# Attention and mixture of experts: the stretch between the last router step and the first expert slot, reordered

## The chip, the cores and the metric

The kernel runs on one core of a Trainium2 chip. A core has a matrix engine (TensorE, PE in the profile, with its weight loads shown as PEld), a vector engine (VectorE, DVE), a scalar engine with function tables (ScalarE, ACT), a general engine (GpSimd, POOL) and an engine that mainly starts transfers (SyncE, SP). Each engine works through its own instructions in order and waits on semaphores for the others. Data lies in on-chip memory of 128 partitions (SBUF); matmuls write into PSUM.

The metric is the time of one execution on the device in microseconds. The profile is of a single execution; the timed runs are others.

## The reference

Everything is float32. There are 32 sequences of 100 tokens with 256 features, and for each sequence 361 context rows with 192 features.

```python
x = x + cross_attention(layernorm(x), ctx)       # softmax over 361 context rows
z = layernorm(x)
shared = gelu(z @ ws1 + bs1) @ ws2 + bs2         # one shared block, all tokens
aff = softmax(z @ Wr + br)                       # 31 experts
vals, idx = top_k(aff, 3)
routed = sum over the 3 chosen experts e of
         aff[e] * (gelu(z @ We1[e] + Be1[e]) @ We2[e] + Be2[e])
x = x + (shared + routed + z)
```

## The kernel before

**Tiles and blocks.** The 3200 tokens are 25 tiles of 128 (`NT`); four tiles make a block, so there are seven blocks, the last with one tile (`BLOCKS`, `TPB = 4`). Inside the part in question the order on the engines is written out by hand (`tc.manual_schedule`, L78): what a line issues stands in its engine's queue where the program puts it.

**Attention and router steps (L796 to L879).** A loop of 37 steps pipelines the sequences: at step i it loads, normalises and transposes one context, forms scores of the one before, weights the one before that. A token tile t is projected out of attention at step `at(t)`, normalised one step later, gets its router logits two steps later (`route_turn`, `route_logits`, `route_choice`) and its slots three steps later (`route_gates`, `route_count`, `route_slots`, `route_scatter`). The last steps, 33 to 36, have no attention left to speak of: step 34 has the logits of tile 23 and the slots of tile 22, step 35 the logits of tile 24 and the slots of tile 23, step 36 the slots of tile 24. `route_count` (L665) counts by matmuls how many earlier tokens chose each expert; for tile 24 it also gives the totals from which `cnt` (31 counts) comes (L685). `route_scatter` writes rows to DRAM by indirect transfers on GpSimd.

**The shared block.** `shared_half(k, f, psum)` (L716) forms one half of the hidden layer of block k: four matmul records with 512 columns into a PSUM tile. `shared_gelu(k)` (L725) applies the gelu to both halves. `shared_mm(t)` (L740) takes tile t through the second matrix, with the experts' second biases by gates as a third matmul (six records of 256 columns), into `pys`; `shared_add(t)` (L750) adds that to the tile. PSUM tiles come from one pool with two tags of four buffers each: `ps_t` ("tp") and `ps_m` ("mm").

**From counts to slots (L887 to L981).** From the 31 counts each expert's number of slots (128 rows each) is formed, `nt_i`, and its running sum, `ends`: a cast into a padded buffer (L898) and five shifted adds between two buffers `runs` (L900 to L904), whose 16 leading zeros were written at the start (L411). From `ends` each of up to 105 slots finds its expert `ei`, the number of slots before that expert `st0`, and its first row (L909 to L925). Two transposes (`p_ec`, L930) turn the expert number and first row of each slot from a column into a row. VectorE makes integers of it (`eT`, read by SyncE's registers, which start the loads of weights and rows) and packs four expert numbers into one word (`epT`, read by TensorE's registers). Then `shared_mm(0)` and `shared_mm(1)` stand on TensorE (L944, L945), while VectorE forms two diagonal matrices; their product with ones (`p_bc`, L954) brings per-slot numbers to all partitions. A one-hot matrix is transposed (`p_oh`), the hidden biases of each slot are picked (`p_b1`), and between these stand the other `shared_mm` and the `shared_add` of block 0.

**Slots.** `fetch` starts the transfers for four slots at a time: weights and scattered rows. After the register loads (`registers`, L1106), `shared_second(1)` does the second matrix of block 1 (L1117); then `run(0, NU)` takes 92 slots: two transposes, eight matmul records, gelu, four more, and an indirect store of the rows. At the end the stored rows are collected and summed, beside the shared blocks 2 to 6.

Of the kernel before, what the change touches and what calls it, by code (L numbers as in the profile page):

```python
# [8 lines left out]
F32 = mybir.dt.float32  # L9
# [4 lines left out]
ALU = mybir.AluOpType  # L14
# [21 lines left out]
def xattn_ffn(  # L36
# [5 lines left out]
    nc = tc.nc  # L42
    P = 128
    EPS = 1e-5
    B, L1, D1 = x.shape
    L2, D2 = ctx_in.shape[1], ctx_in.shape[2]
    E = Wq.shape[1]
    NE, _, INTER = We1.shape
    NG = NE + 1
# [20 lines left out]
    const = ctx.enter_context(tc.tile_pool(name="const", bufs=1))  # L70
# [15 lines left out]
    def ps_t(name):  # L86
        return ps.tile([P, 512], F32, tag="tp", name=name)
# [46 lines left out]
    def load_ctx(b):  # L134
        z = zring[b % ZB]
        full = sum(1 for _, n in CH if n == P)
        nc.sync.dma_start(
            z[:, :full, :D2], ctx_in[b, : full * P, :].rearrange("(c p) d -> p c d", p=P)
        )
        for c in range(full, NCH):  # L140
            s, n = CH[c]
            nc.sync.dma_start(z[:n, c, :D2], ctx_in[b, s : s + n, :])
        ztile[b] = z
# [5 lines left out]
    def load_x(t, n):  # L149
        k, j = divmod(t, TPB)  # L150
        nc.sync.dma_start(
            xb[k][:, j : j + n, :], xf[t * P : (t + n) * P, :].rearrange("(t p) d -> p t d", p=P)
        )
# [18 lines left out]
    b2z = const.tile([P, TPB, D1], F32, tag="b2z", name="b2z")  # L172
# [72 lines left out]
    def ctx_rough(g):  # L245
        n = len(CG[g]) * NCH
        yc[g] = rough(vc[g], n, f"c{n}", f"c{g}")
# [20 lines left out]
    def token_rough(g):  # L268
        n, ts = len(XG[g]), slice(XG[g][0], XG[g][-1] + 1)
        v = small_t(n, f"xv{n}", f"x{g}", 1)  # L270
        pool.tensor_scalar(v, mv1[:, ts, 1], 4.0 * (1.0 + EPS), 4.0 * EPS * EPS, ALU.mult, ALU.add)
        yx[g] = v, rough(v, n, f"x{n}", f"x{g}")
# [94 lines left out]
    def iota_t(shape, name, pattern, base=0, mult=0, pool=const):  # L367
        t_ = pool.tile(shape, F32, tag=name, name=name)
        nc.gpsimd.iota(
            t_, pattern=pattern, base=base, channel_multiplier=mult, allow_small_or_imprecise_dtypes=True  # L370
        )
        return t_
# [4 lines left out]
    iota_p = iota_t([P, 1], "iota_p", [[0, 1]], mult=1)  # L377
# [7 lines left out]
    pool.memset(ones, 1.0)  # L385

    GM = 4
    PAD = 16
    iota0 = iota_t([P, NE], "iota0", [[1, NE]])
    dump = iota_t([P, P], "dump", [[P, P]], base=KTOP * T, mult=1)  # L390
    transposed(wq_sb, KD1, wqT, "q")
# [3 lines left out]
    for t in XG[0]:  # L395
# [5 lines left out]
    token_rstd(0)  # L401

    kk = iota_t([P, GM, KTOP], "kk", [[0, GM], [1, KTOP]])
    one, oh, onesf, *runs = (
        const.tile([P, n], F32, tag=name, name=name)
        for name, n in (("one", NE), ("oh", NG), ("onesf", P), ("run0", PAD + NE), ("run1", PAD + NE))
    )
    for t_ in (one, onesf):
        pool.memset(t_, 1.0)
    for t_ in (oh, b2z, *runs):  # L410
        pool.memset(t_, 0.0)  # L411

    mv2 = const.tile([P, NT, 2], F32, tag="mv2", name="mv2")
# [152 lines left out]
    def clear(k):  # L566
        first_, last_ = k * NE // CLEAR, (k + 1) * NE // CLEAR
        nc.sync.dma_start(
            xse[:, first_:last_, :], none[:, None, :].to_broadcast([P, last_ - first_, XW])
        )  # L570
        if k == 0:
            nc.sync.dma_start(xs_d[NE * T :, :], none)
# [33 lines left out]
    def route_rough(ts):  # L606
        v2[ts[0]] = v2[ts[0]], rough(v2[ts[0]], len(ts), f"m{len(ts)}", f"m{ts[0]}")
# [108 lines left out]
    def shared_half(k, f, psum):  # L716

        n = len(BLOCKS[k]) * P
        ph = phs[k, f] = psum(f"phs_{k}_{f}")
        for c in range(2):  # L720
            nc.tensor.matmul(  # L721
                ph[:, :n], ws1_sb[:, c, f::2], xT[k][:, c, :], start=(c == 0), stop=(c == 1)
            )

    def shared_gelu(k):  # L725
        n = len(BLOCKS[k]) * P
        h = hs[k] = shp.tile([P, 2, 512], F32, tag="hs", name=f"hs_{k}")
        for f in range(2):
            nc.scalar.activation(
                h[:, f, :n], phs.pop((k, f))[:, :n], AF.Gelu, bias=b1c[:, f, NE : NE + 1]  # L730
            )

    def shared_first(k):
        for f in range(2):
            shared_half(k, f, ps_m)
        shared_gelu(k)
# [3 lines left out]
    def shared_mm(t):  # L740
        k, j = divmod(t, TPB)
        h, py = hs[k], ps_t(f"pys_{t}")
        for f in range(2):
            nc.tensor.matmul(  # L744
                py[:, :D1], h[:, f, j * P : (j + 1) * P], ws2_sb[:, f, :], start=(f == 0), stop=False
            )
        nc.tensor.matmul(py[:, :D1], gT[k], b2z[:, j, :], start=False, stop=True)  # L747
        pys[t] = py
# [14 lines left out]
    def at(t):  # L763
        return 1 - (-(t + 1) * P // L1)
# [31 lines left out]
    for i in range(B + 5):  # L796
        now, norm, logits, slots = ([t for t in range(NT) if at(t) == i - d] for d in range(4))
        scattered = [t for t in range(EARLY * TPB) if at(t) == i - 4]
        for b in range(AHEAD - 2, AHEAD + 1) if i == 0 else [i + AHEAD]:
            if b < B:  # L800
                load_ctx(b)
        if i in loads:
            loads[i]()
        if i in xloads:
            load_x(*xloads[i])
        if 1 <= i <= CLEAR:
            clear(i - 1)
        for e in range((i - W2) * NE // (B - W2), min((i + 1 - W2) * NE // (B - W2), NE)) if i >= W2 else ():
            nc.sync.dma_start(w2r[:, e, :], w2v[:, e, :])

        if i + 1 in trstd:
            token_rough(trstd[i + 1])
        if i in trstd:
            token_rstd(trstd[i])
        if norm:
            route_rough(norm)
        if i in crough:
            ctx_rough(crough[i])
        if 2 <= i < B + 2:
            exp_transpose(i - 2)  # L820
        for t in slots:
            route_gates(t)
        if 1 <= i < B + 1:
            scores(i - 1)
        for t in logits:
            route_turn(t)
        for t in slots:
            route_count(t)
            route_slots(t)
            route_scatter(t)  # L830
            if i <= B:
                route_transpose(t)
        if i < B:
            ctx_transpose(i)
        if i in crstd:
            ctx_rstd(crstd[i])
        if i + 1 < B:
            ctx_normalise(i + 1)
        for b in cstats.get(i, ()):
            ctx_stats(b)  # L840
        if i == 0:
            ctx_rough(CGOF[2][0])
        for t in tstats.get(i, ()):
            token_stats(t)
        if norm:
            route_rstd(norm)
        for t in norm:
            route_norm(t)
        if 2 <= i < B + 2:
            weighted(i - 2)  # L850
        for t in projected(i + 2):
            token_norm(t)
        for t in logits:
            route_logits(t)
        for t in projected(i):
            token_project(t)
        for t in projected(i + 1):
            token_transpose(t)
        for t in logits:
            route_choice(t)  # L860
        for t in scattered:
            early_residual(t)
        for t in now:
            project_out(t)
        if now:
            route_var(now)
        if i == 0:
            transposed(wv_sb, KD2, wvT, "v")
        if i == 1:
            bias_cols(wv_sb, KD2, B2, BV, lambda ec: wvT[:, ec, D2:DA], "bvc")  # L870
        if i == 2:
            fold_values()
        if i == 5:
            shared_biases()

        if i == B + 1:
            shared_half(0, 0, ps_t)
        if i == B + 3:
            shared_half(0, 1, ps_t)  # L879
    residual_factors(slice(EARLY * TPB, NT))  # L880
    shared_gelu(0)
    shared_first(1)

    att_ctx.close()

# [3 lines left out]
    def sel_t(shape, name, dt=F32):  # L889
        return sel.tile(shape, dt, tag=name, name=name)  # L890
# [3 lines left out]
    nt_i = sel_t([P, NE], "nt_i", I32)  # L894
    nc.vector.tensor_scalar(nt_i, cnt_i, 7, None, ALU.logical_shift_right)
    ntf = sel_t([P, NE], "ntf")
    nc.vector.tensor_copy(ntf, nt_i)
    nc.vector.tensor_copy(runs[0][:, PAD:], nt_i)  # L898
    cur, step = 0, 1
    while step < NE:  # L900
        nc.vector.tensor_tensor(
            runs[1 - cur][:, PAD:], runs[cur][:, PAD:], runs[cur][:, PAD - step : PAD - step + NE], ALU.add
        )
        cur, step = 1 - cur, 2 * step  # L904
    ends = runs[cur][:, PAD:]
    ind = sel_t([P, NE], "ind")
    ei = sel_t([P, 1], "ei")
    st0 = sel_t([P, 1], "st0")
# [3 lines left out]
    nc.vector.scalar_tensor_tensor(ind, iota0, ei, cnt, ALU.is_equal, ALU.mult, accum_out=nn)  # L912

    j128 = sel_t([P, 1], "j128")
    nc.vector.tensor_tensor(j128, iota_p, st0, ALU.subtract)
    nc.vector.tensor_scalar(j128, j128, float(P), None, ALU.mult)
    start = sel_t([P, 1], "start")
    nc.vector.scalar_tensor_tensor(start, nn, float(-P), j128, ALU.add, ALU.min)
    nc.vector.tensor_scalar(start, start, 0.0, None, ALU.max)
# [20 lines left out]
        nc.vector.scalar_tensor_tensor(ep, e4[:, :, k], float(1 << (BITS * k)), ep, ALU.mult, ALU.add)  # L940
    epT = sel_t([1, P // PACK], "epT", I32)
    nc.vector.tensor_copy(epT, ep)

    shared_mm(0)  # L944
    shared_mm(1)  # L945


    diag = sel_t([P, 2 * P], "diag")
# [249 lines left out]
```

## Time and profile before

| what | us |
|---|---|
| runs, median of 3 (lowest to highest) | 505.77 (505.1 to 506.42) |
| the profiled execution: its time | 503.07 |
| the profiled execution: its span, first to last instruction | 501.2 |
| router steps 34 to 36 and the counts, until `p_ec` starts | up to 245.62 |
| `p_ec` to `p_bc` | 245.62 to 248.43 |
| `p_bc` to the first slot's transposes | 248.43 to 259.15 |

The span is what the trace covers; the time has some 1.9 us more around it. The mean granted TensorE clock over the span is 0.978 of full speed. The first part of the page gives each engine's busy time:

```profile
PE 455.3 (91%) x2952; PEld 397.2 (79%) x2952; DVE 312.4 (62%) x1281; ACT 249.2 (50%) x814; POOL 271.7 (54%) x544
```

A busy TensorE includes matmuls that run at a lower clock. The lines of a timeline below give the start in us from the span's start, the duration in us, the engine and source line, the operation with output and inputs, and in brackets the idle time of that engine just before, with what ended it.

### The profile page before, as it was taken

The numbers are of one execution on the slowest core, as the hardware profiler recorded it, in microseconds if no ns is written. First come the engines' busy times: TensorE is split into PE (matmuls) and PEld (weight loads), VectorE is DVE, ScalarE is ACT, GpSimd is POOL, SyncE is SP. The second block draws the span as 40 slices with busy tenths as digits, with TensorE's granted clock in tenths as the row PEclk, the third lists the DMA queues.
The fourth block names the chain that finished last, engine by engine and source line by source line (L and its number), as shares of the span: only waits on it lengthen the run. The fifth ranks groups of instructions, "written<-read, shape, count | busy, mean of one in ns | idle before, by whom it ended". The sixth has DMA issues, their size and how long they took to land. (4 is left out here: it accounts for less than half of the span.)

```text
span 501.2 us, 10979 instructions
## 1 busy us (share of the span) xinstructions
PE 455.3 (91%) x2952; PEld 397.2 (79%) x2952; DVE 312.4 (62%) x1281; ACT 249.2 (50%) x814; POOL 271.7 (54%) x544
## 2 busy tenths in 40 slices
PE   0989997998998999996999999999999999989964
PEld 0878785977887888885579999999999999966653
DVE  0489998798998887757644444444444434312995
ACT  0357686687877786853414444444444444432100
POOL 3334286877676666667604555555555555553750
PEclk9999999799999999999999999999999999999977
DMA  7864954353645741111387888898888888426982
GB/s 214 237 170 136 281 189 140 113 154 104 190 136 164 234 161 42 66 66 55 123 265 223 270 254 263 267 266 249 269 253 265 257 269 260 152 78 243 406 305 94
DMA packets 67784, 98.79 MB, mean 197 GB/s; under 512 B 8290, under 2 KB 43177, under 8 KB 67721
## 3 DMA queue, kind: packets, MB, share of 16 engines
q1 hardware_dynamic: 56348, 72.60, 50.0%
q0 software_dynamic: 8048, 22.17, 11.6%
q10 hardware_dynamic: 3324, 3.28, 1.9%
q8 instruction: 28, 0.46, 0.4%
q14 instruction: 36, 0.29, 0.2%
HBM read 68.27 MB, written 29.74 MB: 196 GB/s over the span
## 5 line engine op out<-in xcount | busy, mean ns | idle before, releaser
L551 POOL DMA_INDIRECT y_d<-ys,yrow x92 | 88.6, 964 | 100.0 <-ACT ys L1074 43.3
L1058 ACT ACTIVATE hT<-ph,b1t 128x128 f32<-128x128 f32 x184 | 57.7, 364 | 103.6 <-PE ph L1053 95.3
L1053 PE MATMUL ph<-xgT,w 128*128 128x128 f32 x736 | 101.8, 281 | 0.1
L1053 PEld LDWEIGHTS ph<-xgT,w 128*128 128x128 f32 x736 | 94.8, 197 | 0.4 <-DVE xgT L1045 0.3
L1068 PE MATMUL py<-w2r,hT 128*128 x368 | 94.3, 380 | 0.0
L551 POOL DMA_INDIRECT xs_d<-xl,su x75 | 75.1, 1001 | 27.4 <-issue 8.9
L1068 PEld LDWEIGHTS py<-w2r,hT 128*128 128x128 f32 x368 | 62.9, 190 | 4.8
L1076 DVE TENSOR_SCALAR ys<-py,gate 128x256 f32<-128x256 f32 x46 | 22.3, 484 | 65.2 <-PE py L1068 65.2
L1045 DVE COPY xgT<-pg 128x256 f32<-128x256 f32 x92 | 38.6, 421 | 33.5 <-PE pg L1043 33.4
L484 PE MATMUL pss<-z2T,qk 65*100 65x361 f32 (+1 forms) x128 | 44.9, 472 | 1.9 <-ACT qk L448 1.7
L513 PE MATMUL pcx<-exT,z 128*65 128x100 f32 (+3 forms) x384 | 44.3, 266 | 0.1
L513 PEld LDWEIGHTS pcx<-exT,z 128*65 128x65 f32 (+3 forms) x384 | 40.8, 168 | 0.7 <-ACT exT L500 0.6
L1043 PEld LDWEIGHTS pg<-ident,xg 128*128 128x128 f32 x184 | 35.6, 196 | 4.0
L1043 PE MATMUL pg<-ident,xg 128*128 128x128 f32 x184 | 35.5, 277 | 0.0
L744 PE MATMUL pys<-ws_sb,hs 128*128 128x256 f32 x100 | 27.7, 402 | 5.8 <-DVE x L752 4.8
L1139 POOL TENSOR_TENSOR y<-y 128x256 f32<-128x256 f32 x25 | 20.1, 804 | 17.8 <-DMA y<-y_d 12.6
L529 PE MATMUL po<-wvo,cT 128*128 128x257 f32 (+1 forms) x100 | 26.9, 391 | 3.1 <-ACT cT L520 2.8
L444 PE MATMUL pq<-zT,m_sb 128*128 128x128 f32 (+1 forms) x200 | 29.6, 294 | 0.0
L491 ACT ACTIVATE ex<-pss,nm 100x361 f32<-100x361 f32 x32 | 18.0, 563 | 22.0 <-DVE nm L489 18.9
L484 PEld LDWEIGHTS pss<-z2T,qk 65*100 65x100 f32 (+1 forms) x128 | 18.8, 167 | 12.1 <-ACT qk L448 3.3
L744 PEld LDWEIGHTS pys<-ws_sb,hs 128*128 128x128 f32 x100 | 19.7, 201 | 10.7 <-issue 8.0
L237 DVE BATCH_NORM_STATS2 stc<-z 128x6 f32<-128x192 f32 (+1 forms) x96 | 27.8, 345 | 0.0
(229 smaller groups left out, 865.8 us busy)
## 6 DMA issues: line engine op xcount, KB each, us to landing
w<-in_L_ffn_We_dram SPq DMA_DIRECT2D x92, 256.0 KB
xg<-xs_d SPq DMA_DIRECT2D x92, 131.5 KB
y<-y_d SPq DMA_DIRECT2D x25, 384.0 KB
w2r<-in_L_ffn_We_dram SPq DMA_DIRECT2D x31, 256.0 KB
z<-in_ctx_dram SPq DMA_DIRECT2D x32, 192.0 KB
xs_d<-none SPq DMA_DIRECT2D x3, 1052.0 KB
out_dram<-x ACTq DMA_DIRECT2D x6, 512.0 KB
x<-in_x_dram SPq DMA_DIRECT2D x5, 512.0 KB
```

Source lines behind the costliest of these rows:

```text
L237: nc.vector.bn_stats(st[:n, c, :], ztile[b][:n, c, :D2])
L444: nc.tensor.matmul(pq[:m, c * P : (c + 1) * P], m_sb[:, d, s : s + m], z[:, d, :], start=(d == 0), stop=(d == 1))
L484: nc.tensor.matmul(pss[:L1, :L2], qk[:m, a, b * L1 : (b + 1) * L1], z2T[:m, a, :], start=(a == 0), stop=(a == 1),)
L513: nc.tensor.matmul(pw[:m, :L1], z[:n, c, s : s + m], exT[:n, c, :], start=(c == 0), stop=(c == NCH - 1))
L529: nc.tensor.matmul(po[:, : D1 + 1], cT[:m, a, t * P % RING : t * P % RING + P], wvo[:m, a, :], start=(a == 0), stop=(a == 1))
L551: ins = nc.gpsimd.indirect_dma_start(out=dst, out_offset=bass.IndirectOffsetOnAxis(ap=index, axis=0), in_=src, in_offset=None).ins
L744: nc.tensor.matmul(py[:, :D1], h[:, f, j * P : (j + 1) * P], ws2_sb[:, f, :], start=(f == 0), stop=False)
L1043: nc.tensor.transpose(pt[:, c * P : (c + 1) * P], g[:, c::2], ident)
L1045: nc.vector.tensor_copy(xgT[i].rearrange("p c s -> p (c s)"), pt[:, : 2 * P])
L1053: nc.tensor.matmul(ph[:, f * P : (f + 1) * P], w1s[:, c, f::2], z[:, c, :], start=(c == 0), stop=(c == 1))
L1058: nc.scalar.activation(hT[i][:, f, :], ph[:, f * P : (f + 1) * P], AF.Gelu, bias=b1t[:, f, i : i + 1])
L1068: nc.tensor.matmul(py[:, :D1], h[:, f, :], w2f[:, bass.ds(e * (2 * D1) + f * D1, D1)], start=(f == 0), stop=(f == 1),)
```

## The change

Three things are changed.

- **The places of the shared halves.** Half (0, 1) goes from step 35 to step 34, half (1, 0) comes to step 35, and half (1, 1) stays behind the loop, after the gelu of block 0. The second-matrix matmuls of tiles 0 and 1 go from behind `epT` to a place ahead of the gelu of block 1, that is ahead of the counts' instructions and of `p_ec`.
- **The running sum.** The cast and the five shifted adds become one `tensor_tensor_scan` on VectorE over the 31 numbers (state times one, plus the next number). The two padded buffers and their zeroing on GpSimd go.
- **`j128`.** A subtraction and a multiplication become one instruction with two operations.

```diff
-    one, oh, onesf, *runs = (
-        const.tile([P, n], F32, tag=name, name=name)
-        for name, n in (("one", NE), ("oh", NG), ("onesf", P), ("run0", PAD + NE), ("run1", PAD + NE))
+    one, oh, onesf = (
+        const.tile([P, n], F32, tag=name, name=name) for name, n in (("one", NE), ("oh", NG), ("onesf", P))
     )
...
-    for t_ in (oh, b2z, *runs):
+    for t_ in (oh, b2z):
         pool.memset(t_, 0.0)
...
         if i == B + 1:
             shared_half(0, 0, ps_t)
+        if i == B + 2:
+            shared_half(0, 1, ps_t)
         if i == B + 3:
-            shared_half(0, 1, ps_t)
+            shared_half(1, 0, ps_m)
     residual_factors(slice(EARLY * TPB, NT))
     shared_gelu(0)
-    shared_first(1)
+    shared_half(1, 1, ps_m)
+    for t in range(2):
+        shared_mm(t)
+    shared_gelu(1)
...
-    nc.vector.tensor_copy(runs[0][:, PAD:], nt_i)
-    cur, step = 0, 1
-    while step < NE:
-        nc.vector.tensor_tensor(
-            runs[1 - cur][:, PAD:], runs[cur][:, PAD:], runs[cur][:, PAD - step : PAD - step + NE], ALU.add
-        )
-        cur, step = 1 - cur, 2 * step
-    ends = runs[cur][:, PAD:]
+    ends = sel_t([P, NE], "ends")
+    nc.vector.tensor_tensor_scan(ends, one, ntf, 0.0, ALU.mult, ALU.add)
...
-    nc.vector.tensor_tensor(j128, iota_p, st0, ALU.subtract)
-    nc.vector.tensor_scalar(j128, j128, float(P), None, ALU.mult)
+    nc.vector.tensor_scalar(j128, iota_p, st0, float(P), ALU.subtract, ALU.mult)
...
-    shared_mm(0)
-    shared_mm(1)
```

`B` is 32, so `B + 1` to `B + 3` are steps 33 to 35.

More of the change, by code (lines that the diff above doesn't have):

```diff
@@ L387, in xattn_ffn @@
     GM = 4
-    PAD = 16
     iota0 = iota_t([P, NE], "iota0", [[1, NE]])
```

## The prediction

> **What bounds the kernel now.** I first read the windows view over the stages, to see which engine fills each:
>
> ```profile
> 237.30:240.60 3.30, 3.30 (x5) 1.50 (x6) 1.50 (x8) 2.47 (x7) 2.81 (x6) 0.54 0.31 108
> 240.60:245.60 5.00, 4.11 (x15) 1.88 (x13) 3.84 (x25) 2.65 (x5) 4.15 (x9) 1.00 0.26 92
> 259.15:445.90 186.75, 186.61 (x1286) 177.58 (x1285) 83.17 (x316) 79.02 (x229) 95.85 (x178) 1.00 0.82 245
> ```
>
> Columns: the stretch in us, its length, busy us of PE, PEld, DVE, ACT and POOL, then the granted TensorE clock, the DMA share and GB/s. From 259.15 to 445.90 TensorE is busy 186.61 of 186.75 us, so the slot loop ends as much earlier as its first matmul starts. What follows (the last shared blocks, the sums) shifts with it. The question is therefore when TensorE reaches 259.15, and the first row shows something odd on that way: 3.3 us at a clock of 0.54. Next the timeline of PE from the last router step on (start, duration, engine, line, what; idle time before it and its releaser):
>
> ```profile
> 236.65 0.85 PE L630 MATMUL pr<-wr,qk 128*128 128x31 f32 x4 [0.54 <-ACT qk L624]
> 237.31 3.45 PE L721 MATMUL phs<-qk,ws_sb 128*128 128x512 f32 x4
> 240.60 0.30 PE L669 MATMUL pp<-sums,onesf 128*128 128x31 f32 x2
> ...
> 241.02 3.68 PE L721 MATMUL phs<-qk,ws_sb 128*128 128x512 f32 x8
> 245.62 0.38 PE L930 MATMUL p_ec<-ident,both 128*1 128x128 f32 x2 [0.91 <-DVE both L923]
> 245.83 1.03 PE L744 MATMUL pys<-ws_sb,hs 128*128 128x256 f32 x4
> ...
> 248.43 0.68 PE L954 MATMUL p_bc<-diag,onesf 128*128 128x256 f32 x2
> ```
>
> Up to p_ec the order is: half (0,1) of the shared block takes 3.29 us (237.31 to 240.60) where eight such matmuls take 3.5 us a little later, that is 1.75 us a half; the count matmuls of tile 24 wait behind it; DVE then runs the counts; p_ec waits 0.91 us for DVE. From p_ec on, pys 0 and 1 fill PE until p_bc at 248.43 (two times 1.30 us), just when DVE has its `diag` ready. From there to 259.15 PE has one gap, 1.05 us for its register loads. The DVE side of the same stretch:
>
> ```profile
> 241.21 0.25 DVE L681 TENSOR_TENSOR eq<-eq,pp 128x93 f32<-128x93 f32 x1 [2.01 <-PE pp L673]
> ...
> 242.39 0.18 DVE L897 CAST ntf<-nt_i 128x31 f32<-128x31 int32 x1
> 242.48 0.17 DVE L898 CAST run<-nt_i 128x31 f32<-128x31 int32 x1
> 242.69 1.09 DVE L901 TENSOR_TENSOR run<-run 128x31 f32<-128x31 f32 x5
> 243.81 0.25 DVE L909 SCALAR_TENSOR_TENSOR ind<-run,iota_p,one 128x31 f32<-128x31 f32 x1
> ...
> 246.03 0.41 DVE L932 CAST eT<-p_ec 1x256 int32<-1x256 f32 x1 [0.41 <-PE p_ec L930]
> ```
>
> Last, windows of 3.41 us, the length of the shortest spell of half clock here. Its boundaries (86.73, 236.92, 240.33, 482.68) all lie on one grid of 3.413 us:
>
> ```profile
> 83.32:86.73 3.41, 1.90 (x11) 1.09 (x9) 3.04 (x14) 1.74 (x8) 0.22 (x2) 1.00 0.46 122
> 151.58:154.99 3.41, 1.79 (x18) 1.82 (x19) 3.20 (x16) 1.76 (x6) 1.64 (x6) 1.00 0.13 47
> 233.51:236.92 3.41, 1.09 (x8) 0.83 (x8) 2.67 (x13) 1.45 (x7) 2.77 (x7) 1.00 0.21 67
> 236.92:240.33 3.41, 3.41 (x8) 1.86 (x8) 1.50 (x8) 2.20 (x7) 2.90 (x6) 0.50 0.28 99
> ```
>
> The first and third are windows after which the clock fell; the second is one after which it did not. So a window with PE about half busy is the border.
>
> **The change, step by step.**
>
> *Half (0,1) a step earlier.* At step 34 it comes behind the logits of tile 23, at about 233.0, and takes 1.75 us at the full clock which this place has. PE sat idle 1.51 us before the transposes of tile 24 (234.71); these slip to 234.95. That is hidden: ScalarE copies them only at 236.25, behind its gate scaling (L663, 236.04). If this cover were gone it would cost 0.25 us.
>
> *Half (1,0) at step 35* takes the old place of (0,1). With the filler before it, the clock should be full here: logits 0.2 us shorter, the half 1.75 instead of 3.29, together about 1.75 us. Count matmuls, L681 and all behind them come 1.75 us earlier: L681 at 239.45.
>
> *Running sums.* The cast (L898) and five adds (L901) go, a scan comes. From L897's start to L909's start is 1.42 us now. After: 0.22 us to the scan's start (the step between dependent ops in the rows above) and the scan. No scan is in the trace. Nearest row: L901, 191 ns each. [...] Ends: 0.19 by the row, 1.1 if it were as slow as the five adds. I take 0.22; with the step to L909 this saves about 0.9. The j128 merge saves one dependent op, 0.19. Together 1.1: `both` is ready at 245.56 - 1.75 - 1.1 = 242.7.
>
> *pys 0 and 1 ahead of p_ec.* They need the gelu of block 0. ScalarE starts its table load at 239.33, after L663, and that moves by 0.2 only; the two gelus end at about 241.1 and 241.7. PE meanwhile runs half (1,1) from 239.25 to 241.0. So pys 0 and 1 run from 241.1 (with about 0.2 us of wait for the second gelu) to 243.9, and p_ec, ready at 242.7, waits for them until 243.9: 1.7 us earlier than now. The DVE saving of 1.1 us is swallowed whole; it pays nothing unless the pys pair moves away. (This also covers a slow scan up to 1.2 us.)
>
> *Behind p_ec.* eT to the second `diag` stays 2.3 us on DVE, p_ec to p_bc 2.8 us as now. But now PE has nothing in between: after p_ec it idles some 2.55 us, to p_bc at 246.7 (-1.7).
>
> *PSUM turn.* If the four "tp" buffers go round in order of allocation, p_oh takes the buffer of pys 0 and pys 3 that of pys 1, each free only after its shared_add. L964 and three adds run at 249.61 to 250.86: the second add ends 2.08 us after p_bc, where pys 3 started 1.92 after it. Cost 0 to 0.4, I take 0.2, on the path.
>
> *DMA and POOL.* The scatters of tile 24 are bound by POOL and don't move (last issue 245.22, landing 2.4 to 2.8 us after: 248.0). SP starts the weights 1.7 us earlier and would reach the row loads at about 248.6, so that wait stays hidden. Two memsets of 0.14 us go from POOL at 19.1, ahead of 5.4 us of idle: nothing. The const tiles that go are 376 bytes per partition: no cost seen.
>
> Sum without the clock: -1.7 + 0.2 = **-1.5 us**.
>
> **The clock.** [...] The row 83.32 says otherwise: in that window the longest gap at the end was under 1.5 us, PE was busy 1.90 of 3.41, and the clock fell, with 1.79 busy it once did not. Taking "idle over 1.9 us in one window" from my count of the streaming time (0.43 of that window, 0.45 in the one that kept its clock), a gap of 2.55 us makes a window fall for (3.41 + 2.55 - 3.8)/3.41 = 0.63 of the positions of the grid. [...] The price: the next 3.41 us run at half, with PE dense from p_bc on: 2.7 to 3.4 us, half of it lost, 1.35 to 1.7, and the 0.2 of pys 3 disappears in it. I take the row, since it is measured here: -1.7 + 1.6 = **-0.1 us**.
>
> **The cases**, against the profiled execution (span 501.2, 503.07 with what lies around it; the median of the runs is 505.77, 2.7 above, and I carry differences over to it):
>
> - *Forecast, 0.46:* the clock stays full at 237 but falls in the new gap. -0.1 us (-0.5 to +0.5), 505.6.
> - *The clock stays full throughout, 0.27:* -1.5 us, 504.3. For it: the gap is short. Against it: the row 83.32.
> - *Slower: both windows fall, 0.20.* Half (0,1) streams only 1.75 us. A window that starts between 233.7 and 234.75 holds parts of two halves and small matmuls, by my count 1.42 us, 0.42 of it, just under the border. Then half (1,0) is slow as now, p_ec gains only 0.3 to 0.8 us, and the gap still costs its 1.6: +0.8 to +1.3, about 506.9. It decides at 237: a clock of 0.5 in the first matmul of that half. For it: the row 233.51. Against it: the place has twice the work now.
> - *pys 0 and 1 don't hold p_ec up, 0.07:* gelu 0 comes earlier or they run under the counts. p_ec follows DVE, -2.8 + 0.2, about 503.2. Against it: the table load at 239.33.
>
> 0.3% is 1.5 us, about what a measurement of this kernel can tell from no change. Faster than that: half of the second case (0.14), the fourth (0.07), a tail of the first (0.03): 0.24. Slower: the upper third of the third case (0.07) and what I haven't seen in the first (0.08): 0.15. Within: 0.61. The range runs from 503.9 (second case with 0.4 to spare) to 507.2 (third case).
>
> **What would show it.** Half (1,0) in 1.75 us and L681 near 239.4; one scan of about 0.2 us; p_ec released by PE rather than by DVE, near 243.9; a PE gap of about 2.5 us ahead of p_bc and a clock of 0.5 in the 3.4 us behind it. Wrong if p_ec still follows `both`, if the clock is half at 237, or if the slot loop starts over 1 us away from 259.0.

## The result and the profile after

The changed kernel takes 503.82 us (median of 6 runs, 501.61 to 503.99) where the kernel before takes 506.55 (6 runs, 505.1 to 507.35). The ratio is 0.9942 with a 95% interval of 0.992 to 0.9963, that is 2.0 to 4.1 us faster. The forecast was 505.6 us and "within 0.3%"; the result lies just below the range (503.9) and beyond 0.3%. The more runs were made, however, the less this first number stood for the change alone, and that is the main subject below. In the table of experiments the medians are of all runs, while the ratios leave out the slow ones, those more than 1.5% above the fastest run of their kernel (two in filled_2, one each in split, pys_back_2 and pys_ahead).

First the stages of the changed kernel, in the windows view (stretch, length, busy us of PE, PEld, DVE, ACT and POOL, granted clock, DMA share, GB/s):

```profile
238.24:240.04 1.80, 1.80 (x6) 0.87 (x6) 1.43 (x8) 1.02 (x6) 1.50 (x4) 1.00 0.41 150
245.32:248.73 3.41, 1.02 (x6) 0.79 (x5) 2.21 (x11) 0.00 (x0) 2.62 (x6) 1.00 0.50 95
248.73:252.15 3.42, 3.42 (x11) 2.52 (x10) 1.61 (x6) 0.52 (x2) 0.10 (x1) 0.50 0.58 193
258.55:445.30 186.75, 186.60 (x1286) 177.58 (x1285) 83.30 (x317) 78.09 (x228) 95.06 (x177) 1.00 0.83 248
```

The half that the count matmuls wait for now runs at the full clock in 1.80 us. The second row is one 3.41 us window with PE busy 1.02 us, and in the next the clock is 0.50. The slot loop (last row) is as full as before. The timeline of PE in the changed kernel (start, duration, engine, line, what; idle before it and its releaser) puts names to this:

```profile
238.24 1.97 PE L719 MATMUL phs<-qk,ws_sb 128*128 128x512 f32 x4
240.04 0.30 PE L667 MATMUL pp<-sums,onesf 128*128 128x31 f32 x2
...
242.27 1.27 PE L742 MATMUL pys<-ws_sb,hs 128*128 128x256 f32 x4
...
245.10 0.38 PE L926 MATMUL p_ec<-ident,both 128*1 128x128 f32 x2
247.87 0.70 PE L947 MATMUL p_bc<-diag,onesf 128*128 128x256 f32 x2 [2.38 <-DVE diag L945]
248.41 1.58 PE L742 MATMUL pys<-ws_sb,hs 128*128 128x256 f32 x4
...
254.44 1.10 PE L742 MATMUL pys<-ws_sb,hs 128*128 128x256 f32 x4 [0.45 <-issue]
```

The DVE timeline of the changed kernel shows the scan, and the wait of `eT`:

```profile
242.05 0.22 DVE L902 TENSOR_TENSOR_SCAN ends<-one,ntf 128x31 f32<-128x31 f32 x1
...
243.89 0.14 DVE L919 TENSOR_SCALAR both<-ei 128x1 f32<-128x1 f32 x1
...
245.52 0.41 DVE L928 CAST eT<-p_ec 1x256 int32<-1x256 f32 x1 [1.43 <-PE p_ec L926]
```

`both` is ready at 244.03 (243.89 + 0.14), and `p_ec` starts at 245.10, with no idle time of PE ahead of it: PE's own `pys` pair holds it up by 1.07 us.

Starts alone can't be compared between two executions, because they are shifted by what went before. So all times are counted from the first matmul of the first shared half (229.63 before, 230.76 after), from which on the two programs differ, to the first slot's gelu, after which they don't:

| us after that matmul | `both` ready | `p_ec` | `p_bc` | `p_oh` | first slot's gelu |
|---|---|---|---|---|---|
| before | 15.94 | 15.99 | 18.80 | 20.61 | 31.83 |
| after | 13.26 | 14.34 | 17.10 | 19.87 | 31.23 |

This stretch gained 0.60 us in the profiled executions. Yet the span of the changed kernel's profiled execution, 502.1 us, is 0.9 longer than the 501.2 of before, while its median is 2.7 shorter. The stretch alone therefore can't account for the times. The PEclk line of the page (40 slices of the span, granted clock in tenths) shows the other source. Before, in the execution profiled for the forecast:

```profile
PEclk9999999799999999999999999999999999999977
```

The same kernel in another execution (run b_again, span 506.7 us):

```profile
PEclk9989999798998999999799999999999999999997
```

The first lost clock only once before the stretch in question (6.8 us at half clock), the second four times (17.1 us). At the first shared half it was at 233.62 us instead of 229.63: 4 us between two executions of one kernel, before anything that the change touches on PE. The 10.3 us more at half clock can account for half of that, 5.1 us, at most (a `pys` that takes 1.03 us at full clock takes 1.92 there, as in halves_only below).

### The profile page after: what moved, and what is told of

It reads as the page before. It is cut to its first block, busy times and chain, and to the rows that moved or that the text cites. A ratio compares the mean times of both kernels' runs of the same rounds, so it can differ in the third digit from the quotient of the medians.

```text
span 502.1 us, 10970 instructions
## 1 busy us (share of the span) xinstructions
PE 457.4 (91%) x2952; PEld 398.4 (79%) x2952; DVE 311.1 (62%) x1275; ACT 248.7 (50%) x814; POOL 270.6 (54%) x542
## 5 line engine op out<-in xcount | busy, mean ns | idle before, releaser
L511 PE MATMUL pcx<-exT,z 128*65 128x100 f32 (+3 forms) x384 | 45.5, 270 | 0.1
L511 PEld LDWEIGHTS pcx<-exT,z 128*65 128x65 f32 (+3 forms) x384 | 41.9, 172 | 0.6 <-ACT exT L498 0.6
```

The source lines that it names most:

```text
L511: nc.tensor.matmul(pw[:m, :L1], z[:n, c, s : s + m], exT[:n, c, :], start=(c == 0), stop=(c == NCH - 1))
```

## The experiments

The theories, as the expectations name them: **A**, the moved halves pay because they keep the clock up at the last router step. **B**, the shorter chain on DVE pays. **C**, the stretch is worth -0.6 to -1.6 us, and the rest of the first ratio is how the few runs fell. **D**, 0.9942 is what the change does. Each group of runs was on one chip, beside runs of the kernel before on that chip; ratios are to those. They are not quotients of the two medians (for a_fourth that quotient is 1.0043, for no_scan 0.9995). "Late" marks the three chips on which TensorE's signals come late, as shown further down.

| run | what | median us (runs) | before there (runs) | ratio, 95% |
|---|---|---|---|---|
| b_again | before | 504.97 (22) | 505.18 (59) | 0.9993, 0.9976 to 1.001 |
| halves_only | only the halves move | 504.57 (22) | same | 0.9986, 0.9969 to 1.0002 |
| scan_only | only scan and `j128` | 503.8 (22) | same | 0.9972, 0.9954 to 0.999 |
| pys_back | change, `pys` pair behind `p_ec` | 501.85 (6) | same | 0.9917, 0.9884 to 0.9949 |
| a_again | change (late) | 508.48 (14) | 509.0 (43) | 0.9997, 0.9966 to 1.0028 |
| no_scan | change without scan and merged `j128` (late) | 508.73 (14) | same | 0.9977, 0.995 to 1.0005 |
| filled | change, gap filled (late) | 505.85 (6) | same | 0.9931, 0.9906 to 0.9956 |
| split | `pys` 0 ahead, 1 and 2 behind (late) | 508.25 (22) | same | 0.9981, 0.9963 to 0.9999 |
| a_third | change (late) | 510.34 (14) | 509.63 (67) | 1.0003, 0.9976 to 1.0029 |
| pys_back_2 | as pys_back (late) | 506.63 (22) | same | 0.9933, 0.9912 to 0.9955 |
| filled_2 | as filled (late) | 509.17 (22) | same | 0.9988, 0.9962 to 1.0014 |
| pys_ahead | before, only `pys` pair ahead (late) | 511.65 (22) | same | 1.0025, 1.0002 to 1.0048 |
| b_third | before (late) | 509.35 (22) | 509.59 (32) | 0.9998, 0.9976 to 1.0019 |
| a_fourth | change (late) | 511.8 (11) | same | 1.0071, 1.004 to 1.0102 |
| a_sixth | change | 504.05 (22) | 505.03 (27) | 0.9981, 0.9965 to 0.9996 |

b_fourth and a_fifth are one execution each, on the chip of b_third, for their traces: 510.18 and 512.59 us.

### The parts one by one

**Before, once more** (b_again): no edit.

> The kernel before, unchanged, for another profiled execution. Its first profile (span 501.2) lies 3.5 us under its median (506.55, some 504.7 of span). If half-clock windows make the difference (theory A), the span here is near 504.7 and the trace shows more or longer half-clock spells than the 6.8 us in attention and 3.4 us in the router steps of the first, each costing up to 1.7 us; if it is something else (a slower slot loop, transfers), the clock record is like the first and the stretch hT0 to the end (239.7 us) is the longer one.

0.9993: no difference, as it should be. What this run adds is its trace. Its PE timeline shows two windows of half clock on the last router steps, not one:

```profile
241.50 3.76 PE L721 MATMUL phs<-qk,ws_sb 128*128 128x512 f32 x4
...
250.45 0.38 PE L930 MATMUL p_ec<-ident,both 128*1 128x128 f32 x2 [0.88 <-DVE both L923]
```

The half takes 3.76 us, and the logits and counts around it are slow too (first slot's gelu at 32.65). b_fourth shows the same (32.66). So the stretch before costs 31.83 in some executions and 32.65 in others, 0.8 us apart. (b_third lies between, 32.25: one window, but `p_bc` came 0.36 us later.)

**Only the halves** (halves_only). The `pys` pair stays behind `epT`.

```diff
-        if i == B + 3:
+        if i == B + 2:
             shared_half(0, 1, ps_t)
+        if i == B + 3:
+            shared_half(1, 0, ps_m)
...
-    shared_first(1)
+    shared_half(1, 1, ps_m)
+    shared_gelu(1)
```

> Only the halves are moved; pys 0 and 1 stay behind p_ec; running sums and j128 as before. Theory A (the moved halves keep the clock up in the router steps): L679 some 1.75 us earlier or more, p_ec still released by DVE, the pys pair fills the stretch to p_bc, no clock drop there: -1.7 to -3 us against before. Theory B (the shorter DVE chain is what pays): 0 to -0.5 us.

Its PE timeline:

```profile
237.70 1.97 PE L721 MATMUL phs<-qk,ws_sb 128*128 128x512 f32 x4
...
244.54 0.38 PE L933 MATMUL p_ec<-ident,both 128*1 128x128 f32 x2 [2.64 <-DVE both L926]
...
246.62 1.92 PE L744 MATMUL pys<-ws_sb,hs 128*128 128x256 f32 x4
```

The half is fast and `p_ec` comes 1.67 us earlier (14.32). But PE now has nothing to do while DVE still runs five adds, idles 2.64 us, and the clock falls just behind it: the `pys` of tile 1 takes 1.92 us in place of 1.03, and the first slot's gelu comes at 31.76, where it was. In this execution A's gain at one end is lost at the other. A's -1.7 to -3 us was missed: the median's -0.6 can't be told from none.

**Only the scan** (scan_only).

```diff
-    nc.vector.tensor_copy(runs[0][:, PAD:], nt_i)
...
-    ends = runs[cur][:, PAD:]
+    ends = sel_t([P, NE], "ends")
+    nc.vector.tensor_tensor_scan(ends, one, ntf, 0.0, ALU.mult, ALU.add)
...
-    nc.vector.tensor_tensor(j128, iota_p, st0, ALU.subtract)
-    nc.vector.tensor_scalar(j128, j128, float(P), None, ALU.mult)
+    nc.vector.tensor_scalar(j128, iota_p, st0, float(P), ALU.subtract, ALU.mult)
```

> Only the scan and the merged j128, everything else as before. p_ec waits for DVE by 0.9 us before and would then follow the halves of block 1: -0.9 us at p_ec and at p_bc. Theory A: -0.9 us or less in time. Theory B: -2.9 us, all of the measured gain.

The first slot's gelu is at 30.79, 1.04 earlier than before with one slow window likewise at the last router step; the median is 1.4 lower (interval 0.5 to 2.3, which holds A's 0.9 and not B's 2.9). Alone, the scan and the merged `j128` pay in full: `p_ec` comes right behind the halves of block 1, without idle time.

**The change without the scan** (no_scan). The step from the change to this run is shown; `j128` is in two instructions again, too.

```diff
-    ends = sel_t([P, NE], "ends")
-    nc.vector.tensor_tensor_scan(ends, one, ntf, 0.0, ALU.mult, ALU.add)
+    nc.vector.tensor_copy(runs[0][:, PAD:], nt_i)
...
+    ends = runs[cur][:, PAD:]
```

> The changed kernel with the five shifted adds and the two-step j128 back. The prediction's step: pys 0 and 1 stand ahead of p_ec, so VectorE's 1.1 us are swallowed: p_ec at most 0.1 us later, time as the changed kernel within 0.3 us. If the scan pays (theory B): +1 us or more, p_ec released by DVE well behind the pys pair.

`both` is ready 1.03 us later than in the change (14.29 against 13.26), and `p_ec` stands where it stood (14.37 against 14.34). That is direct: within the change the shorter DVE chain moves `p_ec` by 0.03 us. The medians agree, 508.73 against 508.48 for the change on that chip (a_again). A shorter DVE chain pays alone, not within the change.

**The `pys` pair back behind `p_ec`** (pys_back).

```diff
     shared_half(1, 1, ps_m)
-    for t in range(2):
-        shared_mm(t)
     shared_gelu(1)
...
+    shared_mm(0)
+    shared_mm(1)
```

> The changed kernel with pys 0 and 1 put back behind p_ec. By the prediction's sum p_ec then follows DVE (some 2.8 us earlier than before against 1.7 in the changed kernel), the gap of 2.5 us ahead of p_bc is filled and the clock doesn't fall there: -1.1 to -2.7 us against the changed kernel, that is 501.1 to 502.7. If the place of the pair is worth nothing (theory B): the same as the changed kernel, 503.8.

Its PE timeline:

```profile
244.20 0.38 PE L924 MATMUL p_ec<-ident,both 128*1 128x128 f32 x2 [1.66 <-DVE both L917]
244.41 1.03 PE L742 MATMUL pys<-ws_sb,hs 128*128 128x256 f32 x4
...
247.01 0.66 PE L947 MATMUL p_bc<-diag,onesf 128*128 128x256 f32 x2
```

The gap is now ahead of `p_ec`, shorter (1.66 us), and the pair fills the time until `diag`. No clock is lost, and the first slot's gelu comes at 29.15, 2.7 before its place in the kernel before. The median is 3.3 us lower. On another chip (pys_back_2) the ratio repeats:

> The changed kernel with pys 0 and 1 behind p_ec, again, beside the changed kernel on one chip. Its first profile has phs0 to the first gelu 29.15 us and no clock drop there, 2.1 to 2.7 us below the changed kernel's two. Expected: 0.991 to 0.995 against before, 1.5 to 2.7 us below the changed kernel in the median. If the first value (0.9917) was drawn luck: within 0.5 us of the changed kernel.

0.9933, 3.0 us. This is the best version found; it has the diff's halves and scan and leaves out the pair's move. Against the change it was timed on the second chip only, 506.63 against 510.34 (a_third), and there the change suffers from a late signal that this order doesn't (last section). Without one, the traces put it 1.0 us (a_sixth, clock full) to 2.7 us (a_again) ahead.

**The `pys` pair ahead, alone** (pys_ahead): before, with the pair ahead of the gelu of block 1 and the halves and adds as they were.

```diff
-    shared_first(1)
+    for f in range(2):
+        shared_half(1, f, ps_m)
+    for t in range(2):
+        shared_mm(t)
+    shared_gelu(1)
...
-    shared_mm(0)
-    shared_mm(1)
```

> The kernel before with one edit: pys 0 and 1 ahead of p_ec, halves and running sums as before. By the prediction's step the pair then holds p_ec up: the halves of block 1 end 14.9 us behind phs0, p_ec comes at 17.5 instead of 16.0, p_bc at 20.3 instead of 18.8, with a PE gap of 2.4 us between them and the clock falling there in over half of the executions: +1.5 to +2.9 us against before (1.003 to 1.006). If the place of the pair costs nothing: 1.000.

1.0025 (1.0002 to 1.0048), slower by some 1.3 us. One line of its PE timeline and one of its DVE timeline:

```profile
252.21 0.38 PE L934 MATMUL p_ec<-ident,both 128*1 128x128 f32 x2
254.54 0.41 DVE L936 CAST eT<-p_ec 1x256 int32<-1x256 f32 x1 [3.84 <-remote]
```

`both` is ready at 250.64, so the pair holds `p_ec` up by 1.57 us, as in the forecast's step. (`p_ec` itself came at 15.49 and not at 17.5: in this execution the half at the last router step ran at the full clock, in 1.97 us, and `both` was ready at 13.92 instead of 15.94.) But `eT` then starts 2.33 us after `p_ec` instead of 0.42, one of the late signals that the section on 0.9942 shows. So the hold-up is shown without the rest of the change; how much of the 1.3 us it costs by itself is not.

### What the gap costs

**The gap filled** (filled): four matmul records whose result nobody reads stand between `p_ec` and `p_bc`.

```diff
+    fill = ps_m("fill")
+    for c in range(2):
+        nc.tensor.matmul(fill[:, :512], ws1_sb[:, c, 0::2], xT[0][:, c, :], start=(c == 0), stop=(c == 1))
```

> The changed kernel with four extra matmul records (512 columns, result unused, 1.75 us) in TensorE's gap between p_ec and p_bc. If the gap makes the clock fall (row of the trace): no half-clock spell behind p_bc, p_bc still 2.8 us behind p_ec, phs0 to the first gelu 30.2 us, and -0.5 to -0.9 us in the median against the changed kernel. [...]

Its PE timeline:

```profile
250.94 0.38 PE L926 MATMUL p_ec<-ident,both 128*1 128x128 f32 x2
251.16 1.89 PE L942 MATMUL fill<-qk,ws_sb 128*128 128x512 f32 x4
253.80 0.67 PE L951 MATMUL p_bc<-diag,onesf 128*128 128x256 f32 x2 [0.76 <-DVE epT L938]
254.31 1.03 PE L742 MATMUL pys<-ws_sb,hs 128*128 128x256 f32 x4
```

`p_bc` comes at its place in the change (17.22 against 17.15 in a_again, on the same chip), the clock stays full behind it, and the first slot's gelu is at 30.24 against 31.85: the lost clock was worth 1.6 us there. Work for nothing made this stretch shorter. The ratio of 0.9931 can't be put down to that alone: six runs, and 2.6 us below the median of a_again, more than the 1.6 of the traces. Repeated elsewhere (filled_2):

> The changed kernel with 1.75 us of matmuls in the gap ahead of p_bc, again, beside the changed kernel on one chip. Expected by the clock: stretch 30.2 us in every execution, 0.7 to 1.3 us below the changed kernel in the median. If the gap is harmless in most executions: 0 to 0.3 us.

0.9988: not repeated. There `eT` started 2.02 us after `p_ec` and not 0.42 as in filled, so PE still idled 2.35 us behind the filler, and the clock fell (the `pys` of tile 3 took 1.88 us, and 1.03 in filled). The next section follows this up.

**The pair split** (split): tile 0 ahead of `p_ec`, tiles 1 and 2 behind it, the adds in another order.

> pys 0 ahead of p_ec (it fits into the wait for DVE), pys 1 and 2 between p_ec and p_bc, pys 3 and the gate transposes ahead of p_oh and the bias matmuls. If TensorE's order is what bounds this stretch: one pys (1.30 us) goes into idle time, phs0 to the first gelu 28.0 us against 29.16 with the pair behind p_ec, -1.0 to -1.3 us in time against that (501.85), some -4 us against before. If the end of the stretch is set elsewhere (register loads, rows landing): the same 29.2.

0.9981, not to be told from the change (0.9997 on that chip), and the first slot's gelu is at 31.51, not at 28.0. Now 2.04 us of register loads stand bare behind the `p_b` matmuls (1.05 in the trace before), and a half-clock window follows there (23.41 after the first half; the `pys` in it took 1.91 us). The gap had moved to another place.

### Is 0.9942 the change's own?

The changed kernel on four chips:

> The changed kernel, unchanged, with more executions. Theory C (the profiled execution and the first medians of few runs were drawn from a wide spread, and the change itself is worth about what its stretch shows): median 503.5 to 504.2, ratio to before 0.997 to 0.998. Theory D (the first ratio of 0.9942 is the change's own): ratio 0.993 to 0.995 again. The stretch from phs0 to the first slot's gelu: 31.2 us where the clock falls in the gap ahead of p_bc, about 30.2 where it doesn't.

> The changed kernel a third time. Two measurements stand so far: 0.9942 (0.992 to 0.9963) from 6 runs each, and 0.9997 (0.9966 to 1.0028) from 14 against 43. Theory C (stretch worth -0.6 to -1.6 us, the rest drawn from the clock's spells in attention): 0.996 to 0.999. Theory D (the first ratio is the change's own): 0.994 or less.

> The changed kernel beside b_third. Theory C (worth -0.6 to -1.6 us): ratio 0.996 to 0.999 or, with late signals of its own, up to 1.000. Theory D (the first ratio holds): 0.994 or less.

> The changed kernel once more. If this chip signals on time (before near 505): stretch 30.2 to 31.9 us and a ratio of 0.994 to 0.998. If it signals late (before near 509): p_ec's signal 1.9 us after its start, stretch 32.5 us or more, ratio 1.000 to 1.007.

0.9997, 1.0003, 1.0071, 0.9981: D falls, as 0.9942 was seen on none of them, and the interval of a_fourth (1.004 to 1.0102) lies wholly on the other side. C was nearer, but also too simple: it expected one small gain everywhere. Controls and single traces on the chip of a_fourth:

> The kernel before, for a profile on whatever chip this is. If late signals belong to a chip or an execution and not to the order of the change: p_ec or p_bc late by 1 to 1.9 us here too, stretch phs0 to first gelu 33 us or more. If they belong to the pair ahead of p_ec: none, 31.8 to 32.7 us. Ratio 1.000 within 0.3%.

> The kernel before once more, for the signals and the clock: stretch 31.8 (one half-clock spell in the router steps) or 32.6 (two), more only with late signals.

> The changed kernel once more, for the signals and the clock: stretch 30.2 (clock full), 31.2 to 31.9 (it falls in the gap), 32.5 with a late p_ec signal.

The control came out at 0.9998. So the change itself is slower there, by 0.7% (0.4% by the medians), and the traces show where a part of it lies. `p_ec` to `p_bc` takes 4.4 us in a_fourth and in a_fifth, where it was 2.8, and the first slot's gelu comes at 33.66 and 33.37; in b_third and b_fourth it is at 32.25 and 32.66. That is 0.7 to 1.4 us of the 2.2 between the medians; the rest was not found. a_third has the same gap; its PE timeline:

```profile
247.67 0.38 PE L926 MATMUL p_ec<-ident,both 128*1 128x128 f32 x2
252.01 0.70 PE L947 MATMUL p_bc<-diag,onesf 128*128 128x256 f32 x2 [3.96 <-DVE diag L945]
```

And its DVE timeline:

```profile
249.67 0.41 DVE L928 CAST eT<-p_ec 1x256 int32<-1x256 f32 x1 [3.01 <-remote]
```

`p_ec` starts at 247.67 and runs 0.38 us, but `eT`, which waits for it alone, starts 2.00 us after that start, where it is 0.42 in the profile after (245.10 to 245.52). The signal comes late: the update of TensorE's semaphore, for which `eT` waits, stands at 1.98 us in this trace and at 0.40 in the profile after. The gap grows to 3.96 us, and one or two windows of half clock follow (the first `pys` behind `p_bc` takes 1.33 us here and 1.91 in a_fourth). On the chip of a_sixth none of this is there, as its PE timeline shows:

```profile
244.98 0.38 PE L926 MATMUL p_ec<-ident,both 128*1 128x128 f32 x2
247.75 0.70 PE L947 MATMUL p_bc<-diag,onesf 128*128 128x256 f32 x2 [2.38 <-DVE diag L945]
248.28 1.03 PE L742 MATMUL pys<-ws_sb,hs 128*128 128x256 f32 x4
```

The gap is the 2.38 us of the profile after, yet the `pys` behind it take 1.03 us and not 1.58: the clock stayed full. All changes of the clock in one trace lie on a grid of 3.413 us, to 0.02 us, and its position differs from trace to trace. In a_sixth one of its boundaries, 246.09, falls into the gap (windows view, columns as above):

```profile
242.68:246.09 3.41, 2.69 (x13) 1.99 (x12) 1.81 (x13) 1.14 (x2) 2.88 (x6) 1.00 0.26 93
246.09:249.51 3.42, 1.76 (x8) 1.53 (x9) 2.42 (x13) 0.27 (x1) 1.79 (x4) 1.00 0.58 162
```

Neither window was followed by half clock. In the profile after a window starts at 245.32, holds the whole gap, has 1.02 us of work, and the clock falls. a_again is like it (1.00 us of work in the window with the gap). In all the traces, the windows between the first shared half and the first slot's gelu behind which the clock fell have PE busy 1.4 us or less, and those behind which it stayed full 1.6 or more. This is not the exact border: elsewhere the clock fell behind a window with 1.90, in the row 83.32 that the prediction shows.

## Why the prediction was wrong, and where it held

**Half (1,0) at the full clock, counts 1.75 us earlier: held.** 1.80 us against 3.29, `p_ec` 1.65 us earlier (forecast 1.7).

**The scan: held.** The forecast's 0.22 us for the scan was the author's estimate, and no row of before shows it; the scan took 0.22 us in the profile after (L902) and in a_third. `both` is 2.68 us earlier (forecast 2.85). That the `pys` pair swallows the DVE saving was the forecast's least obvious step, and no_scan shows it.

**Behind `p_ec`: held.** `p_ec` to `p_bc` 2.77 us (forecast 2.8), PE idle 2.38 (2.55).

**The PSUM turn, 0.2 us: not seen.** In a_sixth `p_bc` to `p_oh` takes 1.83 us, and 1.81 before.

**The sum without the clock, -1.5 us: held.** a_sixth has the first slot's gelu at 30.16 and filled at 30.24, against 31.83: -1.6 to -1.7.

**The price of the clock, 1.6 us: mis-sized in the profiled execution.** There it was 1.1 (31.23 against a_sixth's 30.16), because 0.6 us of the delay was taken up by the wait for the register loads, 0.45 us in the profile after where it was 1.05 in the profile before:

```profile
253.90 1.10 PE L744 MATMUL pys<-ws_sb,hs 128*128 128x256 f32 x4 [1.05 <-issue]
```

In a_again the price was the full 1.6, and in a_sixth none. The row 83.32, by which the forecast expected the clock to fall, was right for two of these three. A gap of 2.38 us was followed by half clock in the profile after, with 1.02 us of work in the window that holds it, and by none in a_sixth, where a boundary of the grid, 246.09, falls into the gap.

**The step that failed: "-1.7 + 1.6 = -0.1 us", taken against the profiled execution and carried over to the median.** It set one drop of the clock before against one after as if both were fixed. They are not. Before, the stretch was 31.83 in one trace, 32.25 in another (b_third) and about 32.65 in two (b_again, b_fourth). After, where `p_ec`'s signal is on time, it was 30.16, 31.23 and 31.85. The pairs of these give -2.5 to 0.0 us, and all but one lie below -0.1. Repeated with 22 runs against 27 on one chip (a_sixth), the change is 0.9981, or -1.0 us with an interval of -1.8 to -0.2: between the forecast and its second case (-1.5), with the forecast itself just outside. The mis-sized terms are these: two windows before (0.8 us more), which the forecast never priced, and a drop after that costs 0, 1.1 or 1.6 where 1.6 was taken. The forecast had itself put the chance of that drop at 0.63; times 1.6 this is a mean price of 1.0 us (an estimate from these two numbers), and the sum would have been -0.7.

**The carrying over failed too.** The range of 503.9 to 507.2 held only the unknown costs of this stretch, and left out the forecast's own fourth case at 503.2. The runs of the kernel before on one chip go from 502.68 to 508.61. One cause that the traces show is the clock in attention (17.1 us at half clock in b_again, 6.8 in the profile before), which no part of the change touches. It is not the only one: of those runs, the one of 502.68 us and one of 508.12 both have a mean granted clock of 0.978, and what parts them is not known. Three more runs moved the median of the kernel before from 505.77 to 506.55, 0.8 us, where the forecast was -0.1. So to take 0.3% as "about what a measurement of this kernel can tell from no change" was too bold for so few runs. The -2.7 us of the result is more than the largest pair of stretches gives (-2.5). So a part of the miss lies outside the stretch; how much of it is the luck of the draw and how much the chip of that measurement was not settled.

**And one thing was not in it at all:** chips on which the change shows no gain or loses 0.4 to 0.7%. The forecast's slower case put the loss at the last router step; no trace of the changed kernel has a half clock there (the half takes 1.97 us in the profile after, in a_fourth and in a_sixth, and 3.45 before). The part of the loss that the traces show lies in the gap before `p_bc`, which that case took at 2.55 us and which is 3.98 in a_fourth and a_fifth.

## What to carry to other kernels

A gap of 2.4 us on TensorE cost another 1.1 or 1.6 us behind it in two traces and nothing in a third, where a boundary of the 3.41 us grid split it: price such a gap by its chance, before and after, and keep work that can stand anywhere for the wait behind a chain's link, as pys_back does, and not ahead of that link, where it holds the chain up. Before a forecast is carried over to a median, look at the spread of that kernel's runs; here a gain of 1 us took some twenty runs on each side, and two chips gave the change different signs.

## What the runs showed of the hardware

**Late signals from TensorE on some chips.** TensorE's matmuls signal by counting up one semaphore. In the profiles of before and after, and on the chips of b_again and a_sixth, it has an update for each of the some 877 signalling matmuls, and the next update comes within 1.2 us of every one's start. On the chips of a_again, a_third and a_fourth the traces show only 673 to 692 updates for as many matmuls, and 47 to 71 matmuls see none within 1.3 us of their start. The kernel before takes 509.0 to 509.6 us there (medians), and 505.0 to 505.2 on the chips of b_again and a_sixth. The late updates and the longer time go together on all five chips; that one causes the other is not shown.

**They don't hit each order alike.** With the pair ahead of `p_ec`, the late update was that of `p_ec` in six of eight traces there (not in a_again and filled). With `pys` tiles behind it, as in pys_back_2, b_third, b_fourth and split, `p_ec`'s update was on time. That some matmul follows is not enough: filled_2 has the filler right behind `p_ec`, and its update was late. pys_back_2 waited 0.60 us for DVE at `p_oh` and had its first slot's gelu at 29.89, against 32.57 in a_third. Why updates are late or run together, and whether the pair's place decides it, was not tried and stays open.
